# Layers 1 to 3 of a four-layer graph network on one core: whole-array vector passes against tile-by-tile ones over all eight PSUM banks

## The chip, the cores and the metric

The kernel runs on one core of a Trainium2 chip. The metric is the device time of one execution in microseconds (us), and the median of three runs is given. Engines are named as in the profile: PE is the matrix engine (PEld its weight loads), DVE the vector engine, ACT the scalar engine, POOL the GpSimd engine, SP the engine that only issues transfers here. PSUM, where PE writes, has eight banks of 512 floats on each of 128 partitions.

## The reference, cut to what matters

Four layers work on 3327 nodes with 128 features, in float32, all with the same dense 3327 x 3327 matrix `adj`. Each is x = x + layer(relu(layernorm(x))):

```
h = maximum(layernorm(x), 0);  x = x + L0(h, adj, adj, Wq, Wk, Wv, Wo)      # 128 "heads" of softmax attention
h = maximum(layernorm(x), 0);  x = x + L1(h, adj, embed, layer, biases)     # hyperbolic
h = maximum(layernorm(x), 0);  x = x + L2(h, adj, weight, bias)             # hyperbolic, with proj and relu
h = maximum(layernorm(x), 0);  x = x + L3(h, adj, W_in, W_out)

L1: a = f1(h @ embed); y = f2(a (+) embed_bias); u = adj @ y
    out = f3([h, f4(u)] @ layer) (+) layer_bias
L2: the same pattern: h @ weight.T, (+) bias, adj @ y, relu, rescaling
L3: (adj / rowsum(adj)) @ h @ W_in + (adj.T / rowsum(adj.T)) @ h @ W_out
a (+) b = ((1 + 2 a.b + b.b) a + (1 - a.a) b) / (1 + 2 a.b + a.a b.b), row by row
```

Every f multiplies a row by a number that depends on norms of the row alone (square roots, tanh, artanh).

## The kernel before

Node n = p*26 + t sits on partition p in tile t, so an array of all nodes is [128, 26, 128] and a number per node is [128, 26]. Layer 0 (lines 313 to 747) fills most of the time: its exponentials on ACT are in an order written out by hand, and it leaves its result in DRAM (`oT_d`) head by head. It is not part of the change. Everything from line 750 on is written without a fixed order: a scheduler places each instruction on its engine's queue, and each queue then runs in that order.

The end of layer 0 (lines 750 to 779, the output stage) loads `oT_d` two tiles at a time (`ot`, four buffers), divides by the softmax sums on DVE, transposes on PE, multiplies by `Wo`, and adds to `xs`, the array x. While it runs, the weights of the later layers and the first four strips of adj are loaded.

Layers 1 to 3 (lines 782 to 1006) hold every intermediate as a whole array and treat it in whole-array passes. `normed` (line 204) is the layer norm: a sum over each row, a subtraction, a square on ACT, a sum again, a multiplication and a maximum, each over 3328 elements per partition. `transposed` turns h over PE into `hT`, `project` (line 813) multiplies it with a weight, both four tiles at a time into the one bank `ps_t` that is left beside the seven of `aggregate`; `evac` copies each bank out, by ACT and DVE in turn. `sumsq` squares on ACT and sums on DVE. `ball_add` is (+): two passes for a.b, three for the result. `scaled` multiplies each row by its number. The numbers per node are worked out by `Small` in chains of 128x26 instructions on DVE, with square roots, tanh and logarithms on ACT.

`aggregate` (line 822) is adj @ y. Its seven banks collect [128 features, 3327 nodes] over 26 strips of adj, each a transfer of 1.66 MB into one of four buffers, issued by SP and POOL in turn; each strip meets y's tile as seven matmuls. Layer 1 and layer 2 call it once, layer 3 twice: first with the strips of adj transposed (`strip_T`), then with adj's rows (`strip_rows`). In layer 3 each strip is also summed on DVE for the degrees (line 836). Then the banks are copied out to `uT`, and `to_rows` (line 851) transposes back.

Of the kernel before, what the change touches and what calls it, by code (L numbers as in the profile page):

```python
# [10 lines left out]
F32 = mybir.dt.float32  # L11
# [11 lines left out]
P = 128  # L23
# [40 lines left out]
def tiles_of(b):  # L64
    return range(4 * b, min(4 * b + 4, NT))
# [18 lines left out]
def gnn_kernel(ctx: ExitStack, tc: tile.TileContext, x, adj, Wq, Wk, Wv, Wo, embed, layer,  # L84
# [665 lines left out]
    xs = load_x(const)  # L750
    with tc.tile_pool(name="f1", bufs=1) as f1, tc.tile_pool(name="f2", bufs=4) as f2, \
            tc.tile_pool(name="f_ps", bufs=3, space=PSUM) as f_ps:
        wo = f1.tile([P, HD], F32, name="wo")
# [27 lines left out]

    big = ctx.enter_context(tc.tile_pool(name="big", bufs=1))
    wts = ctx.enter_context(tc.tile_pool(name="wts", bufs=1))
    strips = ctx.enter_context(tc.tile_pool(name="strips", bufs=4))
    ps_u = ctx.enter_context(tc.tile_pool(name="ps_u", bufs=1, space=PSUM))
    ps_s = ctx.enter_context(tc.tile_pool(name="ps_s", bufs=1, space=PSUM))

    emb_w = wts.tile([P, D], F32, name="emb_w")
    nc.sync.dma_start(emb_w, embed)
    lay_w = wts.tile([P, 2, D], F32, name="lay_w")  # L790
    nc.sync.dma_start(lay_w, layer.rearrange("(k p) d -> p k d", p=P))
    w_in = wts.tile([P, D], F32, name="w_in")
    nc.sync.dma_start(w_in, W_in)
    w_out = wts.tile([P, D], F32, name="w_out")
    nc.sync.dma_start(w_out, W_out)
    w2T = weight_T(wts, ps_s, weight, "w2T")

    def on_all(v, name):
        o = wts.tile([P, D], F32, name=name)
        nc.sync.dma_start(o, v.unsqueeze(0).to_broadcast([P, D]))  # L800
        return o

    eb = on_all(embed_bias, "eb")
    lb = on_all(layer_bias, "lb")
    hb = on_all(bias, "hb")

    def arr(name):
        return big.tile([P, NT, D], F32, name=name)

    def matT():  # L810
        return big.tile([P, NP], F32, name="hT"), big.tile([P, NP], F32, name="uT")

    def project(lhsT, w, dst):

        for c in range(7):
            ts = tiles_of(c)
            ps = ps_s.tile([P, 4, P], F32, name="ps_t")
            for t in ts:
                nc.tensor.matmul(ps[:, t - 4 * c, :], lhsT[:, t * P:(t + 1) * P], w, start=True, stop=True)  # L819
            evac(dst[:, ts[0]:ts[-1] + 1, :], ps[:, :len(ts), :])  # L820

    def aggregate(y, uT, strip_of, deg=None):
# [3 lines left out]
        pu = [ps_u.tile([P, AW], F32, name=f"pu{c}") for c in range(7)]  # L826
# [10 lines left out]
        by_tile = uT.rearrange("f (t p) -> f t p", p=P)  # L837
        nc.vector.memset(uT[:, N:NP], 0.0)
        for c, w in enumerate(width):
            p0, k = c * AW // NT, w // NT  # L840
            evac(by_tile[:, :, p0:p0 + k], pu[c][:, :k * NT].rearrange("f (p t) -> f t p", t=NT))
        k *= NT
        evac(by_tile[:, 0:w - k, P - 1], pu[6][:, k:w])
# [7 lines left out]
    def to_rows(uT, dst):  # L851
        for c in range(7):
            ts = tiles_of(c)
            ps = ps_s.tile([P, 4, P], F32, name="ps_t")
            for t in ts:
                nc.tensor.transpose(ps[:, t - 4 * c, :], uT[:, t * P:(t + 1) * P], ident)
            evac(dst[:, ts[0]:ts[-1] + 1, :], ps[:, :len(ts), :])

    def scaled(dst, a, s):
        nc.vector.tensor_tensor(dst, a, over_d(s), op=ALU.mult)  # L860

    def row_sum(name, v, pool, tmp):

        o = pool.tile([P, 1], F32, name=name)
        nc.vector.tensor_tensor(tmp, v, v, op=ALU.mult)
        nc.vector.tensor_reduce(o, tmp, axis=AX.X, op=ALU.add)
        return o

    def ball_add(sm, dst, a, tmp, coef, norm, b, y2, least):

        nc.vector.tensor_tensor(tmp, a, over_t(b), op=ALU.mult)
        ab = sm.new()
        nc.vector.tensor_reduce(ab, tmp, axis=AX.X, op=ALU.add)
        xy = sm.mul(coef, ab)
        xn = sm.mul(coef, norm)
        x2 = sm.mul(xn, xn)
        e = sm.ts(xy, 2.0, ALU.mult, 1.0, ALU.add)
        na = sm.ts(e, y2[:, 0:1], ALU.add)
        den = sm.ts(sm.add(e, sm.ts(x2, y2[:, 0:1], ALU.mult)), least, ALU.max)
        rd = sm.recip(den)  # L880
        al = sm.mul(sm.mul(na, coef), rd)
        be = sm.mul(sm.ts(x2, -1.0, ALU.mult, 1.0, ALU.add), rd)
        nc.vector.tensor_tensor(tmp, over_t(b), over_d(be), op=ALU.mult)
        scaled(dst, a, al)
        nc.vector.tensor_tensor(dst, dst, tmp, op=ALU.add)

    brow = wts.tile([P, D], F32, name="brow")


    with tc.tile_pool(name="g1", bufs=1) as g1:  # L890
        sm = Small(g1, "s")
        eb2 = row_sum("eb2", eb, g1, brow)
        lb2 = row_sum("lb2", lb, g1, brow)
        h, tmp = arr("h"), arr("tmp")
        hT, uT = matT()
        normed(sm, xs, h, tmp)
        transposed(ps_s, h, hT)
        hh = sumsq(sm, h, tmp)
        nx = sm.ts(sm.sqrt(hh), L1_EPS, ALU.max)
        s1 = sm.div(sm.artanh(nx, L1_MAX_TANH), nx)  # L900
        a = arr("a")
        project(hT, emb_w, a)
        an = sm.sqrt(sumsq(sm, a, tmp))
        nv = sm.ts(sm.mul(s1, an), L1_EPS, ALU.max)
        c1 = sm.div(sm.mul(sm.act(nv, AF.Tanh), s1), nv)
        y = arr("y")
        ball_add(sm, y, a, tmp, c1, an, eb, eb2, L1_EPS)
        yn = sm.ts(sm.sqrt(sumsq(sm, y, tmp)), L1_EPS, ALU.max)
        scaled(y, y, sm.div(sm.artanh(yn, L1_MAX_TANH), yn))
        aggregate(y, uT, strip_T)  # L910
        u = arr("y")
        to_rows(uT, u)
        uu = sm.sqrt(sumsq(sm, u, tmp))
# [5 lines left out]
        w1, w2 = arr("a"), arr("y")  # L919
        project(hT, lay_w[:, 0, :], w1)  # L920
        project(uT, lay_w[:, 1, :], w2)
        scaled(w2, w2, cu)
        nc.vector.tensor_tensor(w1, w1, w2, op=ALU.add)
        wn = sm.sqrt(sumsq(sm, w1, tmp))
        nv2 = sm.ts(sm.mul(sz, wn), L1_EPS, ALU.max)
        c2 = sm.div(sm.mul(sm.act(nv2, AF.Tanh), sz), nv2)
        o1 = arr("y")
        ball_add(sm, o1, w1, tmp, c2, wn, lb, lb2, L1_EPS)
        nc.vector.tensor_tensor(xs, xs, o1, op=ALU.add)


    with tc.tile_pool(name="h1", bufs=1) as h1:
        sm = Small(h1, "s")

        def clip_of(n):

            return sm.ts(sm.recip(n), L2_MAXNORM, ALU.mult, 1.0, ALU.min)

        b2 = row_sum("b2", hb, h1, brow)
        b2w = sm.new()  # L940
        nc.vector.tensor_copy(b2w, b2.to_broadcast([P, NT]))
        bn = sm.ts(sm.sqrt(b2w), L2_MIN_NORM, ALU.max)
        bt = sm.act(bn, AF.Tanh)
        bc = sm.mul(sm.div(bt, bn), clip_of(sm.ts(bt, L2_MIN_NORM, ALU.max)))
        nc.vector.tensor_scalar(hb, hb, bc[:, 0:1], None, op0=ALU.mult)
        hb2 = row_sum("hb2", hb, h1, brow)

        h, tmp = arr("h"), arr("tmp")
        hT, uT = matT()
        normed(sm, xs, h, tmp)  # L950
        transposed(ps_s, h, hT)
        xn = sm.ts(sm.sqrt(sumsq(sm, h, tmp)), L2_MIN_NORM, ALU.max)
        a = arr("a")
        project(hT, w2T, a)
        an = sm.ts(sm.sqrt(sumsq(sm, a, tmp)), L2_MIN_NORM, ALU.max)
        th = sm.act(sm.mul(sm.div(an, xn), sm.artanh(xn, L2_MAX_TANH)), AF.Tanh)
        c1 = sm.mul(sm.div(th, an), clip_of(sm.ts(th, L2_MIN_NORM, ALU.max)))
        y = arr("y")
        ball_add(sm, y, a, tmp, c1, an, hb, hb2, L2_MIN_NORM)
        yn = sm.ts(sm.sqrt(sumsq(sm, y, tmp)), L2_MIN_NORM, ALU.max)  # L960
        pf = clip_of(yn)
        pn = sm.ts(sm.mul(yn, pf), L2_MIN_NORM, ALU.max)
        scaled(y, y, sm.mul(sm.div(sm.artanh(pn, L2_MAX_TANH), pn), pf))
        aggregate(y, uT, strip_T)
        u = arr("a")
        to_rows(uT, u)
        un = sm.ts(sm.sqrt(sumsq(sm, u, tmp)), L2_MIN_NORM, ALU.max)
        t1 = sm.ts(sm.act(un, AF.Tanh), L2_MIN_NORM, ALU.max)
        p2 = clip_of(t1)
        n2 = sm.ts(sm.mul(t1, p2), L2_MIN_NORM, ALU.max)  # L970
        k2 = sm.mul(sm.mul(sm.div(sm.artanh(n2, L2_MAX_TANH), n2), p2), sm.div(t1, un))
        nc.vector.tensor_scalar(u, u, 0.0, None, op0=ALU.max)
        rn = sm.ts(sm.mul(k2, sm.sqrt(sumsq(sm, u, tmp))), L2_MIN_NORM, ALU.max)
        t3 = sm.act(rn, AF.Tanh)
        k3 = sm.mul(sm.mul(sm.div(t3, rn), k2), clip_of(sm.ts(t3, L2_MIN_NORM, ALU.max)))
        scaled(u, u, k3)
        nc.vector.tensor_tensor(xs, xs, u, op=ALU.add)


    with tc.tile_pool(name="i1", bufs=1) as i1:  # L980
        sm = Small(i1, "s")
        h, tmp = arr("h"), arr("tmp")
        normed(sm, xs, h, tmp)
        vT, uT = matT()
        deg, degT = sm.new(), sm.new()
        nc.vector.memset(deg, 1.0)
        nc.vector.memset(degT, 1.0)
# [5 lines left out]
        aggregate(h, uT, strip_T, degT)  # L993
        aggregate(h, vT, strip_rows, deg)
        r_in, r_out = over_degree(deg), over_degree(degT)
        zi, zo = arr("a"), arr("y")
        project(uT, w_in, zi)
        project(vT, w_out, zo)
        scaled(zi, zi, r_in)
        scaled(zo, zo, r_out)  # L1000
        nc.vector.tensor_tensor(zi, zi, zo, op=ALU.add)
        nc.vector.tensor_tensor(xs, xs, zi, op=ALU.add)
        for p0, p1 in pieces(P - 1):
# [33 lines left out]
```

## Time and profile before

| what | us |
|---|---|
| median of 3 runs (lowest to highest) | 11689.48 (11686.55 to 11691.01) |
| the profiled execution's own time | 11686.64 |
| its span, first to last instruction | 11684.9 |
| layer 0 up to its last result store | 10572.9 |
| layer 0's output stage, to the last addition to `xs` | 103.3 |
| four aggregations, PE busy 294.2 in layers 1 and 2 and 292.5 in layer 3 | 586.7 in all |

The profiled execution is 2.8 us below the median. Its page lists the share of each engine over the whole span, of which layer 0 is nine tenths; the change is read from the last tenth, by stretches of time between the aggregations.

### The profile page before, as it was taken

The numbers are of one execution on the slowest core, as the hardware profiler recorded it, in microseconds if no ns is written. First come the engines' busy times: TensorE is split into PE (matmuls) and PEld (weight loads), VectorE is DVE, ScalarE is ACT, GpSimd is POOL, SyncE is SP. The second block draws the span as 40 slices with busy tenths as digits, with TensorE's granted clock in tenths as the row PEclk, the third lists the DMA queues.
The fourth block names the chain that finished last, engine by engine and source line by source line (L and its number), as shares of the span: only waits on it lengthen the run. The fifth ranks groups of instructions, "written<-read, shape, count | busy, mean of one in ns | idle before, by whom it ended". The sixth has DMA issues, their size and how long they took to land.

```text
span 11684.9 us, 195477 instructions
## 1 busy us (share of the span) xinstructions
PE 10973.1 (94%) x72798; PEld 3492.3 (30%) x72798; DVE 4850.4 (42%) x7190; ACT 10392.7 (89%) x13945; POOL 1887.6 (16%) x3247
## 2 busy tenths in 40 slices
PE   4699999999999999999999999999999999996578
PEld 2222222222222222222222222222222222224334
DVE  5344443444444443444444444444443333335335
ACT  3699999999999999999999999999999999993100
POOL 4211112111121111211112111121111211110000
PEclk7799999999999999999999999999999999997789
DMA  8755555555455544555555545455544544442356
GB/s 249 241 91 91 90 91 105 92 88 94 85 110 88 93 85 82 107 90 90 90 90 105 93 87 93 84 112 88 93 85 81 101 81 78 82 78 104 129 198 240
DMA packets 651406, 1242.72 MB, mean 106 GB/s; under 512 B 185527, under 2 KB 527424, under 8 KB 633820
## 3 DMA queue, kind: packets, MB, share of 16 engines
q1 hardware_dynamic: 609016, 1100.82, 48.4%
q0 software_dynamic: 41440, 129.30, 3.7%
q8 instruction: 588, 9.63, 0.4%
q14 instruction: 362, 2.97, 0.1%
HBM read 1082.90 MB, written 146.60 MB: 105 GB/s over the span
## 4 chain that ended last, share of the span: by engine, by line
ACT 80%; PE 8%; issue 5%; DVE 3%; DMA 1%; POOL 0%; SPq 0%; DVEq 0%; POOLq 0%; ACTq 0%
ACT e L641 80%; PE pu L833 5%; PE S L629 1%; PE ps_t L819 1%; PE po L649 1%; PE ps_y L778 0%; DVE S L623 0%; DVE s L201 0%; ACT tmp L199 0%; DMA ot<-oT_d 0%; DVE y L860 0%; PE ps_t L774 0%; DMA a<-adjT 0%; DVE s L149 0%; DMA QS<-qS_d 0%
## 5 line engine op out<-in xcount | busy, mean ns | idle before, releaser
L641 ACT ACTIVATE e<-S 128x952 f32<-128x952 f32 (+3 forms) x13589 | 10106.8, 916 | 8.9 <-PE S L629 7.8
L623 DVE COPY S<-a 128x476 f32<-128x476 f32 (+1 forms) x5824 | 3739.3, 655 | 5992.5 <-ACT e L641 5733.8
L649 PE MATMUL po<-e,VA 128*9 128x476 f32 (+1 forms) x46592 | 5738.7, 565 | 15.6 <-DVE OS L661 2.6
L629 PE MATMUL S<-QS,KT 64*128 64x476 f32 (+1 forms) x23296 | 5080.3, 443 | 111.2 <-DMA a<-adjT 18.8
L629 PEld LDWEIGHTS S<-QS,KT 64*128 64x128 f32 x23296 | 2277.8, 184 | 5376.8 <-DVE S L623 2703.1
L665 POOL DMA_DIRECT2D oT_d<-OS x896 | 470.7, 531 | 5599.7 <-DVE OS L661 5531.4
L649 PEld LDWEIGHTS po<-e,VA 128*9 128x9 f32 x46592 | 695.0, 89 | 1790.6 <-issue 1691.3
L550 POOL TENSOR_SCALAR QS<-QS 32x476 fp32r<-32x476 f32 (+1 forms) x1344 | 781.9, 582 | 1330.5 <-DMA QS<-qS_d 732.2
L123 ACT COPY uT<-pu 128x494 f32<-128x494 f32 (+2 forms) x12 | 6.3, 528 | 457.1 <-PE pu L833 456.5
L833 PE MATMUL pu<-strip,y 128*128 128x494 f32 (+2 forms) x728 | 294.2, 567 | 92.8 <-DVE y L860 92.8
L833 PE MATMUL pu<-strip,h 128*128 128x494 f32 (+2 forms) x728 | 292.5, 565 | 66.8 <-DVE h L213 66.8
L560 POOL COPY VA<-VR 128x832 f32<-128x832 f32 x224 | 198.4, 886 | 969.5 <-DMA VR<-v_d 740.9
L571 POOL TENSOR_TENSOR a<-a,shb 128x476 f32<-128x476 f32 (+1 forms) x182 | 213.0, 1205 | 240.4 <-DMA a<-adjT 203.9
L836 DVE TENSOR_REDUCE s<-strip 128x1 f32<-128x3327 f32 (+1 forms) x52 | 188.0, 3618 | 106.7 <-DMA strip<-adjT 60.6
L833 PEld LDWEIGHTS pu<-strip,y 128*128 128x128 f32 (+1 forms) x728 | 139.3, 192 | 247.1 <-issue 142.2
L275 DVE STREAM_TRANSPOSE cols<-rows 128x416 f32<-128x416 f32 x208 | 203.5, 983 | 21.0 <-DMA rows<-in_adj_dram 14.1
L833 PEld LDWEIGHTS pu<-strip,h 128*128 128x128 f32 (+1 forms) x728 | 138.9, 191 | 220.2 <-issue 141.1
L661 DVE COPY OS<-po 128x476 f32<-128x476 f32 (+1 forms) x224 | 145.6, 650 | 52.3 <-PE po L649 45.9
L831 POOL DMA_DIRECT2D strip<-adjT x39 | 20.7, 532 | 791.9 <-PE pu L833 764.0
L123 ACT COPY hT<-pu 128x494 f32<-128x494 f32 (+1 forms) x4 | 2.2, 546 | 143.0 <-PE pu L833 143.0
L221 PE MATMUL ps_t<-ident,h 128*128 128x128 f32 x78 | 20.3, 428 | 114.9 <-DVE h L213 100.9
L127 DVE COPY uT<-pu 128x494 f32<-128x494 f32 (+2 forms) x12 | 6.8, 577 | 290.8 <-PE pu L833 290.4
(153 smaller groups left out, 1745.5 us busy)
## 6 DMA issues: line engine op xcount, KB each, us to landing
KT<-kS_d SPq DMA_DIRECT2D x1792, 208.0 KB
KT<-kS_d SPq DMA_DIRECT2D x1792, 104.0 KB
VR<-v_d SPq DMA_DIRECT2D x224, 416.0 KB
strip<-adjT POOLq DMA_DIRECT2D x39, 1663.5 KB, 7.6
strip<-adjT SPq DMA_DIRECT2D x36, 1663.5 KB
QS<-qS_d SPq DMA_DIRECT2D x3072, 14.9 KB
QS<-qS_d SPq DMA_DIRECT2D x1536, 29.8 KB
adjT<-cols SPq DMA_DIRECT2D x26, 1664.0 KB
```

Of the source, the lines that this page charges most:

```text
L275: nc.vector.transpose(self.cols[:, t0:t0 + NQ, 32 * j:32 * j + 32], self.rows.rearrange("p (x t) -> p t x", t=NT)[:, t0:t0 + NQ, :])
L550: nc.gpsimd.tensor_scalar(QS[b][r0:r0 + 32, j + 1, :w], QS[b][r0:r0 + 32, j, :w].bitcast(F32), -1.0, 0.0, op0=ALU.mult, op1=ALU.add)
L560: nc.gpsimd.tensor_copy(VA[(c * NG + g) % 2][:, :, :, 0:H], v.rearrange("p j (t e) -> p t j e", e=H))
L571: nc.gpsimd.tensor_tensor(a[:, :w], a[:, :w], shift[:, :w], op=ALU.subtract)
L623: touch(u, [r], nc.vector.tensor_copy(bank(u, r), adj_of[c][2 * q + r][:, :w]))
L629: x = nc.tensor.matmul(bank(u, r), KT[b][64 * r:64 * r + 64, max(0, j - 1), q * P:(q + 1) * P], QS[b][64 * r:64 * r + 64, j, :w], start=Fa ...
L641: touch(u, range(a, b), nc.scalar.activation(e[:, a:b, :w], S[u % 3][:, lo + a:lo + b, :w], AF.Exp, scale=2.0))
L649: nc.tensor.matmul(po[32 * j:32 * j + H + 1, :w], VA[k % 2][:, 2 * q + r, j, :], e_of[u, j][:, at, :w], start=(q == 0 and r == 0), stop=(q ...
L661: nc.vector.tensor_copy(o[:, :w], po[:, :w])
L665: nc.gpsimd.dma_start(oT_d[:, d * N + c * CW:d * N + c * CW + w], o[32 * j:32 * j + H + 1, :w])
L833: nc.tensor.matmul(pu[c][:, :w], y[:m, t, :], s[:m, c * AW:c * AW + w], start=(t == 0), stop=(t == NT - 1))
L836: nc.vector.tensor_reduce(deg[:m, t:t + 1], s[:m], axis=AX.X, op=ALU.add)
```

## The change

It rewrites layers 1 to 3 and moves their preparations ahead of layer 0's output stage. Part by part:

- Weights and biases are loaded, and all that depends on the biases alone is computed, before the output stage. `embed`, `layer` and `weight` get one more column, the product with the bias (`with_product`), so that a.b comes out of the projection.
- `layer_norm` replaces `normed`: per tile `bn_stats` and `bn_aggr` on DVE, then per tile one ACT instruction relu(r*x + off).
- All eight banks are shared by `bank_u`: projections and transposes rotate over seven, the eighth takes norms. Squares are summed over features by a matmul with a column of ones (`column_squares`), or per three or four tiles (`row_squares`).
- (+) and the scalings become per-tile instructions `scalar_tensor_tensor` (`add_scaled`), and the norm of the sum is computed from numbers per node (`sum_norm`) rather than from the array.
- h @ layer[:128] is projected before layer 1's aggregation; the sums of the strips in layer 1 give `degT`; layer 3 takes adj's rows first, and the projection of that result runs inside its second aggregation, by `also`.
- The last projection, the addition to x and the store go in seven groups.

```diff
+    eb, lb, hb = on_all(embed_bias, "eb"), on_all(layer_bias, "lb"), on_all(bias, "hb")
+    ...
+        bc = sm.mul(sm.div(bt, bn), clip_of(sm, sm.ts(bt, L2_MIN_NORM, ALU.max)))
+        nc.vector.tensor_scalar(hb, hb, bc[:, 0:1], None, op0=ALU.mult)
+    emb_w = wts.tile([P, D + 1], F32, name="emb_w")
+    ...
+        with_product(lay_w[i], lb)
+    with_product(emb_w, eb)
+    ...
+        w_raw = f1.tile([P, D], F32, name="w_raw")
+        nc.sync.dma_start(w_raw, weight)
+        ...
         wo = f1.tile([P, HD], F32, name="wo")
...
-    ps_u = ctx.enter_context(tc.tile_pool(name="ps_u", bufs=1, space=PSUM))
-    ps_s = ctx.enter_context(tc.tile_pool(name="ps_s", bufs=1, space=PSUM))
+    banks_u = ctx.enter_context(tc.tile_pool(name="banks_u", bufs=1, space=PSUM))
+    def next_bank():
+        turn[0] += 1
+        return bank_u(turn[0] % 7)
+    def layer_norm(sm, xs, h):
+        mv = sm.pool.tile([P, NT, 2], F32, name="mv")
+        for t in range(NT):
+            st = part.tile([P, 6], F32, name="st", bufs=8)
+            nc.vector.bn_stats(st, xs[:, t, :])
+            nc.vector.bn_aggr(mv[:, t, :], st)
+        r = sm.recip(sm.sqrt(sm.ts(mv[:, :, 1], LN_EPS, ALU.add)))
+        off = sm.mul(sm.ts(mv[:, :, 0], -1.0, ALU.mult), r)
+        for t in range(NT):
+            nc.scalar.activation(h[:, t, :], xs[:, t, :], AF.Relu, scale=r[:, t:t + 1], bias=off[:, t:t + 1])
+    def column_squares(sm, of, dst_of=None):
+        o = sm.new()
+        ps = bank_u(7)
+        for c in range(7):
+            ts = tiles_of(c)
+            src = of(c)
+            sq = part.tile([P, 4 * P], F32, name="sq")
+            nc.scalar.activation(sq[:, :len(ts) * P], src, AF.Square)
+            if dst_of is not None:
+                nc.vector.tensor_copy(dst_of(c), src)
             for t in ts:
+                nc.tensor.matmul(ps[:, t:t + 1], sq[:, (t - ts[0]) * P:(t - ts[0] + 1) * P], ones,
+                                 start=True, stop=True)
+        nc.vector.tensor_copy(o, ps[:, :NT])
+        return o
+    def add_scaled(dst, a, s, b):
+        nc.vector.scalar_tensor_tensor(dst, a, s, b, op0=ALU.mult, op1=ALU.add)
...
-        y = arr("y")
-        ball_add(sm, y, a, tmp, c1, an, eb, eb2, L1_EPS)
-        yn = sm.ts(sm.sqrt(sumsq(sm, y, tmp)), L1_EPS, ALU.max)
-        scaled(y, y, sm.div(sm.artanh(yn, L1_MAX_TANH), yn))
-        aggregate(y, uT, strip_T)
+        al, be = ball_sum(sm, c1, aa, ab, eb2, L1_EPS)
+        yn = sm.ts(sum_norm(sm, al, be, aa, ab, eb2), L1_EPS, ALU.max)
+        f = sm.div(sm.artanh(yn, L1_MAX_TANH), yn)
+        al, be = sm.mul(al, f), sm.mul(be, f)
+        y = arr("y")
+        for t in range(NT):
+            nc.scalar.activation(y[:, t, :], a[:, t, 0:D], AF.Copy, scale=al[:, t:t + 1])
+            add_scaled(y[:, t, :], eb, be[:, t:t + 1], y[:, t, :])
+        w1 = arr("w", D + 1)
+        project(hT, lay_w[0], lambda ts, ps: evac(w1[:, ts[0]:ts[-1] + 1, :], ps))
+        pu, width = aggregate(y, strip_T, degT)
...
-        ball_add(sm, o1, w1, tmp, c2, wn, lb, lb2, L1_EPS)
-        nc.vector.tensor_tensor(xs, xs, o1, op=ALU.add)
+        al, be = ball_sum(sm, c2, ww, w1[:, :, D], lb2, L1_EPS)
+        for t in range(NT):
+            add_scaled(xs[:, t, :], w1[:, t, 0:D], al[:, t:t + 1], xs[:, t, :])
+            add_scaled(xs[:, t, :], lb, be[:, t:t + 1], xs[:, t, :])
...
-        aggregate(h, uT, strip_T, degT)
-        aggregate(h, vT, strip_rows, deg)
-        ...
-        project(uT, w_in, zi)
-        project(vT, w_out, zo)
-        scaled(zi, zi, r_in)
-        scaled(zo, zo, r_out)
-        nc.vector.tensor_tensor(zi, zi, zo, op=ALU.add)
-        nc.vector.tensor_tensor(xs, xs, zi, op=ALU.add)
+        r_out = over_degree(degT)
+        pu, width = aggregate(h, strip_rows, deg)
+        vT = matT("hT")
+        by_tiles(pu, width, vT)
+        r_in = over_degree(deg)
+        pu, width = aggregate(h, strip_T, also={
+            3 * c + 4: lambda c=c: add_projected(c, bank_u(7), vT, w_out, r_out) for c in range(7)})
+        uT = matT("uT")
+        by_tiles(pu, width, uT)
+        for c in range(7):
+            add_projected(c, next_bank(), uT, w_in, r_in)
+            ...
+            nc.sync.dma_start(out[0:(P - 1) * NT].rearrange("(p t) d -> p t d", t=NT)[:, ts[0]:ts[-1] + 1, :],
+                              xs[0:P - 1, ts[0]:ts[-1] + 1, :])
```

`ball_sum` and `sum_norm` are some fifteen and ten 128x26 instructions; `add_projected` is four matmuls into one bank and four `add_scaled` into xs.

## The prediction

> **What bounds the kernel now.** The page's first lines say ACT 89% and PE 94%, but nine tenths of the span are layer 0, which the change leaves alone. So I first cut the span at the aggregations (busy time in nine stretches), then asked for the groups of instructions by form after layer 0, for the chain of waits, and last for PE's granted clock in short stretches.
>
> ```profile
> core 0: us, PE busy (x) PEld busy (x) DVE busy (x) ACT busy (x) POOL busy (x), PEclk, DMA share, GB/s
> 10572.90:10676.20 103.30, 78.89 (x633) 75.41 (x633) 75.32 (x88) 17.09 (x28) 10.32 (x13) 0.87 0.66 227
> 10676.20:10777.40 101.20, 21.05 (x78) 16.21 (x78) 68.25 (x114) 24.95 (x24) 0.00 (x0) 0.51 0.00 0
> 10777.40:10924.80 147.40, 147.25 (x364) 69.69 (x364) 2.02 (x3) 1.80 (x4) 6.93 (x13) 0.99 0.81 287
> 10924.80:11116.00 191.20, 54.92 (x208) 43.48 (x208) 126.11 (x227) 49.48 (x54) 0.00 (x0) 0.51 0.03 11
> 11116.00:11263.00 147.00, 146.93 (x364) 69.63 (x364) 2.04 (x4) 1.76 (x3) 6.87 (x13) 0.99 0.81 288
> 11263.00:11340.50 77.50, 5.56 (x26) 3.41 (x26) 59.71 (x84) 18.65 (x18) 0.00 (x0) 0.54 0.07 25
> 11340.50:11633.00 292.50, 292.48 (x729) 139.16 (x730) 179.05 (x65) 3.93 (x7) 12.69 (x24) 0.99 0.77 280
> 11633.00:11685.00 52.00, 20.23 (x105) 16.94 (x103) 19.34 (x13) 4.33 (x8) 0.00 (x0) 0.64 0.10 33
> ```
>
> Read it by rows: in the aggregations PE is busy all the time, so nothing but PE sets their length. In the gaps between them (101.2, 191.2, 77.5, 52.0, together 422 us) no engine is full. DVE leads with 60 to 77%, and the rest is one engine waiting for the other. The change is about these 422 us and the 103 us of the output stage before them. The prices:
>
> ```profile
> L201 DVE TENSOR_REDUCE s<-tmp 128x26 f32<-128x3328 f32 x13 | 47.0, 3619 | 30.9 <-ACT tmp L199 30.9
> L149 DVE TENSOR_TENSOR s<-s,s 128x26 f32<-128x26 f32 x142 | 25.2, 182 | 3.9 <-ACT s L176 0.3
> L199 ACT ACTIVATE tmp<-y 128x3328 f32<-128x3328 f32 x3 | 8.9, 2976 | 27.2 <-DVE y L885 27.1
> L860 DVE TENSOR_TENSOR y<-y,s 128x3328 f32<-128x3328 f32 x4 | 14.5, 3625 | 0.5 <-ACT y L123 0.3
> L779 DVE TENSOR_TENSOR xs<-xs,ps_y 128x128 f32<-128x128 f32 x26 | 7.4, 285 | 7.2 <-PE ps_y L778 7.1
> L176 ACT ACTIVATE s<-s 128x26 f32<-128x26 f32 x28 | 6.3, 225 | 56.2 <-DVE s L161 44.6 <-DVE s L149 11.5
> ```
>
> A whole-array pass costs 3.62 us on DVE and 2.98 on ACT; a tile costs 0.285 on DVE, so 26 tiles 7.4, twice the pass. Tiles win only where they remove passes or let engines overlap. Dependent 128x26 steps start 0.22 us apart in the timeline; a step over ACT and back takes 0.47.
>
> ```profile
> 10714.00:10732.00 18.00, 13.63 (x52) 11.63 (x52) 2.15 (x4) 1.75 (x3) 0.00 (x0) 0.50 0.01 1
> 10777.40:10781.00 3.60, 3.55 (x5) 1.61 (x6) 0.00 (x0) 0.00 (x0) 0.00 (x0) 0.50 0.00 0
> 10781.00:10785.00 4.00, 4.00 (x12) 1.97 (x11) 0.00 (x0) 0.00 (x0) 0.00 (x0) 1.00 0.00 0
> 11633.00:11645.30 12.30, 7.47 (x54) 6.13 (x52) 2.46 (x6) 2.58 (x5) 0.00 (x0) 1.00 0.00 1
> ```
>
> PE's clock: a projection at 76% busy stays at half clock (2.08 us for four tiles), 3.6 us without a pause bring full clock (1.16), and once there 61% busy keeps it.
>
> **1. Output stage, earlier ready time.** Before, PE starts its first `ot` at 10592.7, stalls from 10603 to 10616 for later `ot` loads, then runs full at 5.57 us for two tiles. After, by the order of the queues: SP issues eight small transfers first (about 5.5 us by their rows before), then `ot`, strip, `ot`, strip, `w_raw`, `wo`; on POOL's queue too a strip now stands before the second `ot`. PE's first instruction is the transpose of `w_raw`, whose memory is that of the bias chain's numbers, so its load waits for the scaling of `hb` on DVE; that stands behind the sum of the first strip (3.62), which waits for that strip. Four strips, four `ot` and weights are 12 MB; the stretch 10574 to 10600 moved about 0.39 MB per us, so they are in by about 10607. PE starts at 10608. The stall at the fifth `ot` is then gone, since four are there. PE alone would end at 10608 + 13 x 5.57 = 10680. DVE has more: nine pairs of reciprocal and product 36.3 (1.75 + 2.28), 26 copies 15.6, 26 additions 6.5, three strip sums 10.7, the products with the biases 2.5, and 26 pairs of `bn_stats` and `bn_aggr`. These last are not in the trace. Nearest row: a 128x128 sum, 0.28, and a small step, about 0.12 when it waits for nothing: 0.40, so 10.4. Bounds: 0.2 (both hidden in each other's start) and 1.0 (three passes over a tile). Sum 82 us, 10690, and 5 for the last pair's way through PE: statistics complete at 10695.
>
> **2. Layer 1 up to its aggregation.** Small chain 3.0. Then 26 relus on ACT with two per-partition operands. The rows give (2976 - 225)/3302 = 0.83 ns an element, so 0.31 a tile, 8.1 in all. [...] At 10708 the squares can start (they follow the relus in ACT's queue), and hT's copies follow the squares. From here PE has ones (52 loads and matmuls), `emb_w` and `layer` (52 each): 21.5 us at full clock (0.127 an instruction with one column, 0.29 a tile), 39.5 at half. DVE has 7 copies, 9 copies of a, 9 sums, 33 small steps, 5 copies of w: 22. The small steps after the norm of a stand in DVE's queue behind the last copy of w, so all of this counts. PE has no pause at half clock and should warm up; I take 27, between 22 and 39.5. Then square root 1.7, tanh and c1 1.6, `ball_sum` 2.4, `sum_norm` 1.3, square root and artanh 5.5 (6.0 before from 10767.8 to 10773.8). That is 12.5. The first aggregation waits for y's first tile only, 0.9, where before it waited for three whole passes. Start: 10695 + 3 + 10.4 + 27 + 12.5 + 0.9 = 10749, against 10777.4. **-28.**
>
> **3. Between aggregations 1 and 2** (191.2 before), counted from the last matmul: copies out 1.0; square and ones 7.3, numbers to `cu` 2.7 (sum 11); DVE then has 26 `add_scaled` 7, 9 sums 4.1, about 45 small steps 7: 18 (29); last square and sum 1, chain to `al` 5.5 (35.5); 52 `add_scaled` on xs at 0.27, 14 (49.5); statistics 10.4 (60); chain 3 (63); relus 10.4 (73.4); first square, ones and projection with DVE's 14 us beside, 19.6 (93); artanh of h's norm, clips and the chains of layer 2, 19 (112); y 0.9 (113). What goes: six squares and sums (6.6 each), two `ball_add` with five passes each, the passes of `normed`, and h @ `layer`, which now lies before the aggregation. **-78.**
>
> **4. Between 2 and 3** (77.5): copies out 1; transposes, relu, 14 squares on ACT at 0.54 and the ones 12 (13); chain 13, as before from 11286 to 11299; `add_scaled` 7 (33); statistics 10.4 (43.4); small chain 3 and, in its midst in DVE's queue, the sums of the first four strips, 14.1, exactly as before: here nothing is gained, as adj's rows come first and need their own degrees (60.5); first relu and matmul 0.9 (61.4). **-16.**
>
> **5. The aggregations.** 26 projections inside the last one: 26 x 0.29 at full clock, **+7.5**. The strip sums of layer 1, 22 x 3.62 = 80 us of DVE, lie beside 147 us of PE, where DVE had 2 us of work; a buffer is free when both have read it, and DVE reads earlier. Cost nothing; layer 3 before shows the same sums under PE at 292.48 of 292.50. If DVE came late, POOL and SP would issue strips late and PE would wait: see the rivals.
>
> **6. End** (from PE's last matmul to the end 51.8): copies out 1.0, first group 1.2, 26 additions at 0.3, 7.8, last transfer 3.8 (7.8 before from the last issue, of which 1.7 MB at the rate above are 4.4): 14. POOL's seven one-partition stores go beside. **-38.**
>
> Sum: -28 - 78 - 16 + 7.5 - 38 = -152.5. From the profiled execution's own 11686.6: 11534. The median of the runs shown stands 2.8 above it: **11537**.
>
> **Rivals.** (a) PE stays at half clock in the projections: 39.5 for 27 in layer 1, about +8.5 in layer 2: 11537 + 21 = 11558. [...] (b) The output stage is later, since a load is held by in-order DVE: every us that `wo` comes after 10608 is a us; with `ot`s also queued behind strips, +20: 11557. (c) All overlaps are good: `bn` 0.25, layer 1 bound by DVE's 22, output stage 6 earlier: about 11512. (d) The statistics take 1.0 a tile, 78 tiles: +47, 11584. (e) Slower: the fixed price of a small instruction. About 338 per-tile instructions stand one after another on the path (26 relus and 52 statistics in layer 1's start, 156 in gap 3, 78 in gap 4, 26 at the end), reckoned at some 0.3. From 0.75 us each the 152 us are eaten; at 0.8 the time is about 11706. Against it stand 26 rows of 0.285 at the same size on DVE; for it, that two-tensor forms with a per-partition scalar are not in the trace at this size.
>
> **How the numbers follow.** Likeliest 0.47, (a) 0.17, (b) 0.1, (c) 0.15, (d) 0.08, (e) 0.03. Own range of the likeliest: 11520 to 11552 (10 us on the output stage, 6 on `add_scaled`, 8 on the clock). With (a), (b), (c) and most of (d): 11505 to 11582. This kernel's measurement can tell about 0.2%, 23 us, from no change; only (e) comes near, so faster 0.96, same 0.015, slower 0.025.
>
> **What would show it.** Right: gaps of about 113 and 61 us before PE's second and third aggregation, the first starting near 10749, PE still full inside all four, the last additions 10 us behind PE's last matmul, `bn` pairs near 0.4 and relus near 0.4. Wrong: pauses of PE inside the first aggregation, a granted clock of 0.5 through all projections, `add_scaled` above 0.4 us, or an output stage that ends after 10710.

## The result, and the profile after

The changed kernel takes 11600.4 us (median of 4 runs, 11598.5 to 11601.2), the kernel before 11689.0 (11686.6 to 11691.0): a ratio of 0.9924, 95% interval 0.9907 to 0.9941. That is 88.6 us faster where 152 were forecast; the time lies 63 us above the forecast and 18 above the upper end of its range. The profiled execution took 11601.2 us, with a span of 11599.4.

The span is cut at the aggregations as before; each row gives the busy time of each engine in one stretch (columns in the first line). The stretches between aggregations are called gaps.

```profile
core 0: us, PE busy (x) PEld busy (x) DVE busy (x) ACT busy (x) POOL busy (x), PEclk, DMA share, GB/s
10574.60:10702.50 127.90, 79.16 (x633) 74.73 (x633) 103.34 (x179) 20.36 (x33) 10.32 (x13) 0.83 0.53 183
10702.50:10758.10 55.60, 38.22 (x182) 32.10 (x183) 28.85 (x129) 27.94 (x60) 0.00 (x0) 0.62 0.00 1
10758.10:10906.60 148.50, 148.42 (x364) 69.97 (x364) 88.81 (x50) 8.61 (x28) 6.96 (x13) 0.98 0.80 285
10906.60:11017.60 111.00, 47.19 (x235) 41.04 (x235) 71.35 (x350) 44.37 (x86) 0.00 (x0) 0.58 0.05 18
11017.60:11166.00 148.40, 148.39 (x364) 69.94 (x364) 9.17 (x28) 8.60 (x27) 6.90 (x13) 0.98 0.80 285
11166.00:11227.70 61.70, 14.34 (x79) 14.02 (x79) 46.99 (x169) 16.71 (x28) 0.00 (x0) 0.56 0.09 32
11227.70:11526.20 298.50, 298.47 (x780) 144.35 (x780) 92.01 (x60) 13.47 (x32) 12.75 (x24) 0.99 0.76 274
11526.20:11599.40 73.20, 6.07 (x52) 5.88 (x52) 7.08 (x28) 0.45 (x1) 3.44 (x7) 0.56 0.06 24
```

The two gaps between aggregations are what was forecast, 111.0 and 61.7 us, and PE is full in all aggregations. The last row is the surprise: 73.2 us after PE's last matmul of the aggregations, against 51.8 before and 14 forecast. No engine does anything in most of it: PE has 6 us, DVE 7. By step, the differences add up to the change of the span: start of the first aggregation 10777.4 to 10758.1, -19.3; gaps -80.2 and -15.8; aggregations +8.5; end +21.4; together -85.4 of the 85.5.

The stretch after the last addition, and the transfers to `out` by their queue (durations in ns as least, median, most, then the first and last start):

```profile
11535.20:11599.40 64.20, 0.00 (x0) 0.00 (x0) 0.00 (x0) 0.00 (x0) 0.49 (x2) 0.50 0.06 25
```
```profile
L1113 SPq DMA_DIRECT2D out_dram<-xs x7: 241/10061/10129, 11529.3 to 11574.4; - x7
L1115 POOL DMA_DIRECT2D out_dram<-xs x7: 484/487/517, 11529.6 to 11535.2; - x7
```

POOL has issued its seven one-partition stores by 11535.7. SP's seven stand 10.06 us (median) in the queue. The DMA share is 0.06, one sixteenth, and it is the mean busy share of 16 engines: that could be one engine that is always busy, or sixteen that are seldom busy. The trace's packet records tell which. Of the 67.8 us in which SP's queue moves packets, exactly one packet is in flight for 64.3, and never more than two; a packet of 2 KB takes 79 ns. So one engine carries 25 GB/s and fifteen stand still. 254 KB a group at that rate is the 10 us that each store takes. Before, the same 1.7 MB left in 8.6 us, with sixteen packets in flight for most of the transfer:

```profile
11676.30:11684.90 8.60, 0.00 (x0) 0.00 (x0) 0.00 (x0) 0.00 (x0) 0.00 (x0) 0.50 0.61 198
```

What differs is the first dimension of the transfer. The kernel before stores 112 and then 15 partitions (`pieces`); the change stores 127 at once. The experiments ask first whether it is that, or POOL's stores, or the smaller pieces; then what sets the rest of the time.

### The profile page after: what moved, and what is told of

Read it like the earlier page. It is cut to its first block, busy times and chain, and to the rows that moved or that the text cites. A ratio compares the mean times of both kernels' runs of the same rounds, so it can differ in the third digit from the quotient of the medians.

```text
span 11599.4 us, 196522 instructions
## 1 busy us (share of the span) xinstructions
PE 10982.6 (95%) x72980; PEld 3500.4 (30%) x72980; DVE 4766.2 (41%) x7583; ACT 10411.4 (90%) x14091; POOL 1895.5 (16%) x3254
## 4 chain that ended last, share of the span: by engine, by line
ACT 80%; PE 8%; issue 6%; DVE 2%; DMA 1%; POOL 0%; SPq 0%; DVEq 0%; POOLq 0%; ACTq 0%
ACT e L641 79%; PE pu L941 5%; PE S L629 1%; PE po L649 1%; DVE S L623 0%; PE pu L893 0%; DMA ot<-oT_d 0%; PE ps_y L837 0%; DVE xs L928 0%; PE pu L916 0%; PE pu L904 0%; POOL a L571 0%; DVE s L149 0%; DMA KT<-kS_d 0%; DVE s L944 0%
## 5 line engine op out<-in xcount | busy, mean ns | idle before, releaser
L275 DVE STREAM_TRANSPOSE cols<-rows 128x416 f32<-128x416 f32 x208 | 203.2, 982 | 21.4 <-DMA rows<-in_adj_dram 14.1
L407 ACT CAST st_k<-st_q 128x1664 fp32r<-128x1664 f32 x16 | 53.7, 3378 | 75.9 <-DMA st_q<-kraw_d 58.0
L944 DVE TENSOR_REDUCE s<-strip 128x1 f32<-128x3327 f32 (+1 forms) x26 | 93.9, 3616 | 59.7 <-DMA strip<-in_adj_dram 59.7
L944 DVE TENSOR_REDUCE degT<-strip 128x1 f32<-128x3327 f32 (+1 forms) x26 | 94.0, 3616 | 54.0 <-DMA strip<-adjT 54.0
## 6 DMA issues: line engine op xcount, KB each, us to landing
QS<-qS_d SPq DMA_DIRECT2D x3072, 14.9 KB
```

Of the source, the lines that this page charges most:

```text
L275: nc.vector.transpose(self.cols[:, t0:t0 + NQ, 32 * j:32 * j + 32], self.rows.rearrange("p (x t) -> p t x", t=NT)[:, t0:t0 + NQ, :])
L944: nc.vector.tensor_reduce(deg[:m, t:t + 1], s[:m], axis=AX.X, op=ALU.add)
```

## The experiments

All times are medians of four runs; the kernel before measured 11689.3, 11688.3 and 11689.1 beside the three groups of four.

**1. The store cut at 112** (`e1_split_store`).

```diff
-            nc.sync.dma_start(out[0:(P - 1) * NT].rearrange("(p t) d -> p t d", t=NT)[:, ts[0]:ts[-1] + 1, :],
-                              xs[0:P - 1, ts[0]:ts[-1] + 1, :])
+            for p0, p1 in pieces(P - 1):
+                nc.sync.dma_start(out[p0 * NT:p1 * NT].rearrange("(p t) d -> p t d", t=NT)[:, ts[0]:ts[-1] + 1, :],
+                                  xs[p0:p1, ts[0]:ts[-1] + 1, :])
```

> The changed kernel, but each of the seven stores to `out` on SP's queue is cut at partition 112 (112 and 15 partitions) as all other transfers of 127 partitions in the kernel are. Theory A (a transfer whose first dimension is 127 goes to one DMA engine, so the last 73 us are 1.69 MB at 24 GB/s): the stores keep up with the additions, the last work is POOL's last one-partition store, landing about 5 us after 11535; time about 11541 us, 59 below the changed kernel. Theory B (POOL's seven one-partition stores are what ends late): no change, 11600. Theory C (seven store groups of 2 KB pieces instead of one with 13 KB pieces are slow in themselves, and there are now fourteen): 11600 or later.

Measured: 11541.5 us (11540.0 to 11543.9), ratio to before 0.9873 (0.9857 to 0.9890). Its end, in two stretches:

```profile
11526.20:11535.20 9.00, 6.07 (x52) 5.88 (x52) 6.81 (x26) 0.00 (x0) 3.43 (x7) 0.98 0.40 117
11535.20:11540.40 5.20, 0.00 (x0) 0.00 (x0) 0.00 (x0) 0.00 (x0) 0.00 (x0) 0.50 0.42 132
```

The last matmul of its aggregations ends at 11525.4, so the end is now 15.0 us long, with POOL's stores and the 2 KB pieces still there. Theories B and C fall; 59 of the 63 us that were missing are in this one line of code.

**2. The kernel before, with its two stores of 112 and 15 made one of 127** (`e2_before_127`).

```diff
-        for p0, p1 in pieces(P - 1):
+        for p0, p1 in ((0, P - 1),):
```

> The kernel before with one edit: its store of 112 and its store of 15 partitions at the end become one store of 127 partitions (13 KB per partition); the one-partition store stays. Theory A: 1.69 MB at 24 GB/s, 66 to 70 us from the issue at 11676.3 instead of 8.6, so 57 to 62 us slower than before, 11746 to 11751, ratio about 1.005. Theories B and C: no change, since POOL has no store here and the pieces are as long as before.

Measured: 11745.5 us (11743.1 to 11751.6), ratio 1.0049 (1.0032 to 1.0065), 56 us slower than before, for the 57 to 62 of theory A: A again, from the other side. Its last stretch:

```profile
11678.70:11744.50 65.80, 0.00 (x0) 0.00 (x0) 0.00 (x0) 0.00 (x0) 0.00 (x0) 0.50 0.06 26
```

One engine again, with pieces of 13 KB: the length of the pieces is not it.

**3. The cut at 124** (`e3_124_3`): the edit of 1 with `((0, 124), (124, 127))` for `pieces(P - 1)`.

> As the changed kernel with the seven stores cut at partition 124 (124 and 3 partitions). [...] By this rule each of the seven groups takes 254 KB at 4 x 24 = 97 GB/s, 2.6 us, more than the 1.03 us between two groups: end at about 11529 + 17.8 + 2 = 11549, so about 11551 us, 49 below the changed kernel and some 10 above the cut at 112. Rival A2 (whatever is not a multiple of 16 goes to one engine): 11600. Rival A3 (only a prime number is slow, all others take 16 engines): 11541.

Measured: 11554.3 us (11552.6 to 11557.5), ratio 0.9885 (0.9869 to 0.9902); 13 above the cut at 112, 46 below the changed kernel. Busy share in tenths and GB/s of the transfers in 40 slices from 11529 to the end:

```profile
DMA  0222222222331222222222222222222221000000
GB/s 11 75 62 87 83 100 102 102 105 77 81 59 26 55 86 86 79 97 100 107 100 100 107 100 100 107 100 100 103 100 100 75 73 48 5 0 0 14 0 0
```

A quarter of the engines, at most 107 GB/s, four times 25; four packets are in flight for 14 of 20.6 us. A2 and A3 both fall. The expectation's four engines for 124, its "4 x 24", were an assumption that no earlier run shows; with it the forecast of 11551 is right to 3 us. The packets of SP's queue can also be counted. Seven stores of 127 rows are 889 packets of data, and beside them stand 7 packets of 4 bytes in the changed kernel, 49 = 7 x (4 + 3) with the cut at 124, and 217 = 7 x (16 + 15) with the cut at 112. Read as one per engine and store, which is a reading, that is one engine for 127, four and three for 124 and 3, sixteen and fifteen for 112 and 15. What was in flight at once fits it for three of them: one packet for 127, four for 124, and sixteen in the kernel before, whose stores of 112, 15 and 1 have 32 = 16 + 15 + 1 such packets.

**4. Store once, as before** (`h1_store_once`): the changed kernel with the loop's stores taken out and the three stores of the kernel before after the loop.

> The changed kernel with the end of the kernel before: no store in the loop of additions, and after it the three stores of 112, 15 and 1 partitions. From the changed kernel's trace the last addition ends at about 11534.9; from there 8.6 us as before: span 11543.6, time about 11545, some 3.5 above the cut in seven groups. So the overlap of stores and additions is worth 3 to 4 us if the cut is right. Rival: nothing at all (below 1 us), as the last group's store still has to be issued and to land.

Measured: 11543.2 us (11542.2 to 11544.8); from PE's first matmul of the last projection to the end 2.3 us more than with seven cut groups, by the two profiles. The ranges of the two times overlap. So letting stores and additions overlap is worth about 2 us at best, and its uncut form cost 57.

**5. Weights first** (`e5_weights_first`): experiment 1, and

```diff
+    w_raw = wts.tile([P, D], F32, name="w_raw")
+    nc.sync.dma_start(w_raw, weight)
+    wo = wts.tile([P, HD], F32, name="wo")
+    nc.sync.dma_start(wo, Wo)
     eb, lb, hb = on_all(embed_bias, "eb"), on_all(layer_bias, "lb"), on_all(bias, "hb")
...
-        w_raw = f1.tile([P, D], F32, name="w_raw")
-        nc.sync.dma_start(w_raw, weight)
...
-        wo = f1.tile([P, HD], F32, name="wo")
-        nc.sync.dma_start(wo, Wo)
```

> The cut at 112, and `w_raw` and `wo` in memory of their own, loaded first on SP's queue in the output stage, ahead of the biases, so that PE no longer waits for DVE's bias chain (in the changed kernel PE stood still from 10574 to 10612). Theory (each us that PE starts earlier in the output stage is a us, until DVE's own 103 us of work fill it): the first transposes of `ot` start near 10596 instead of 10616, DVE has no idle time after its first `ot`, statistics complete about 7 us earlier, time about 11534 (7 below the cut alone). Rival (DVE's work or the landing of the `ot` loads already sets the end of the stage): within 2 us of the cut alone.

Measured: 11542.2 us (11540.4 to 11546.3), no gain. By one profile each, PE's first `ot` comes 17.5 us after layer 0's last copy instead of 42.7, but layer 1's first relu 127.2 after it instead of 129.1. The rival holds: PE's start is not what sets the stage's end. (Part of the missing gain lies elsewhere: see the gap at the end of experiment 7.) Its trace has POOL's later `ot` loads wait 58.9 us for PE to let a buffer go.

**6. Degree sums of the first four strips, later.** Tied to the first tile of the aggregation's left side, in layer 3 (`f1_late_sums_l3`), in layer 1 (`f2_late_sums_l1`), and in both with early weights (`f3_late_weights`) or without (`g1_both_ties`), each on top of experiment 1:

```diff
             if deg is not None:
+                if t < 4:
+                    nc.vector.tensor_copy(deg[:m, t:t + 1], y[:m, 0, 0:1])
                 nc.vector.tensor_reduce(deg[:m, t:t + 1], s[:m], axis=AX.X, op=ALU.add)
```

> The cut at 112, and in layer 3 the sums of the first four strips of adj's rows are tied to the first tile of h: one element of h is copied into the sum's place first, so that DVE can't take them up in the midst of the layer norm's small steps. Theory (step 4 of the prediction: these 14.1 us stand on the path between aggregations 2 and 3): gap of 47 to 48 us instead of 61.6, time about 11527, 14 below the cut alone. Rival (the layer norm's way over ACT or PE's clock sets the gap, and DVE would wait in that time anyway): gap above 58, within 4 us of the cut alone.

> The cut at 112, and in layer 1 the sums of the first four strips of adj's columns are tied to the first tile of y in the same way, so they leave the output stage and lie beside PE's first aggregation. Theory (DVE's own work sets the end of the output stage, which is why earlier weights brought nothing): DVE's busy time there falls from 103 to 89 us, `w_raw` and `wo` come 3.6 us earlier, first relu 8 to 14 us earlier, time 11528 to 11534. Rival (the loads of `ot` pace the stage): within 3 us of the cut alone. Check on the cost: PE must stay full in the first aggregation, 148.4 us.

> Both ties (layers 1 and 3), and `w_raw` and `wo` loaded first. If DVE sets the output stage, the early weights bring something only together with the late sums: DVE then has 89 us of work from about 10590, and waits for the third `ot`, which lands behind four strips near 10605. Theory: 14 from layer 3, 14 to 18 from the output stage against the cut alone: 11510 to 11514. Rival (weights early bring nothing with or without the sums): the sum of the two single changes, 11514 to 11520.

> The cut at 112 and both ties of degree sums (layers 1 and 3), weights as in the changed kernel. The single ones measured -12.3 and -3.4 us against the cut alone. Theory 1 (the early weights of the kernel with both ties cost as much as the tie in layer 1 brought): the two add up, about 11525 to 11526. Theory 2 (the 3.4 of layer 1 were chance in the order of the queues): 11529, as with the tie of layer 3 alone.

Measured, against the 11541.5 of experiment 1: layer 3 alone 11529.2 (11526.0 to 11531.9), -12.3; layer 1 alone 11538.1 (11534.4 to 11541.2), -3.4; both 11526.6 (11524.0 to 11528.6), -14.9, about the sum; both with early weights 11531.2 (11530.2 to 11531.9), -10.3, worse than both without them and outside both of its expectations. The groups of runs come from different chips, on which the kernel before differs by 1 us. For layer 3 the cause shows in DVE's timeline of the changed kernel (start, duration in us), just before the third aggregation:

```profile
11211.21 3.61 DVE L944 TENSOR_REDUCE s<-strip 128x1 f32<-128x3327 f32 x1
11215.17 3.61 DVE L944 TENSOR_REDUCE s<-strip 128x1 f32<-128x3327 f32 x1
11218.95 3.60 DVE L944 TENSOR_REDUCE s<-strip 128x1 f32<-128x3327 f32 x1
11222.83 3.60 DVE L944 TENSOR_REDUCE s<-strip 128x1 f32<-128x3327 f32 x1
```

and in that of the kernel with the tie:

```profile
11209.95 0.27 DVE L945 COPY s<-h 128x1 f32<-128x1 f32 x3 [0.56 <-ACT h L874]
11210.15 10.66 DVE L946 TENSOR_REDUCE s<-strip 128x1 f32<-128x3327 f32 x3
```

In the first, four sums stand between the layer norm's small steps and hold back the relus. In the second they begin 0.2 us after PE's aggregation (11209.98) and lie beside it. The second aggregation's start to the third's is 197.6 us instead of 210.1. In layer 1, 14 us less of DVE's work in the output stage brought 3.4 us alone and 2.5 beside the other tie, with ranges that overlap. In its one profile the first relu stands 7.8 us earlier than in that of experiment 1; but `f1_late_sums_l3`, whose output stage has the code of experiment 1, shows it 5.8 earlier as well, so single profiles of this stage spread by that much and the times decide. DVE's amount of work sets at most a small part of it. PE stays full in the first aggregation (148.3 us with both ties).

**7. Which load comes first in the output stage.** Strips after tile 6 of xs (`f4_all`, with the last row's stores on SP); six buffers for `ot` with early weights (`g2_six_ot_weights`); six buffers alone (`g3_six_ot`), where the strips' memory falls on the output stage's and they load after the last `ot`:

```diff
 # f4_all, on top of f3_late_weights
+            if deg is degT and t < 4:
+                nc.vector.tensor_copy(s[:, 0:1], xs[:, 6, 0:1])
 # g2_six_ot_weights, on top of f3_late_weights; g3_six_ot, on top of g1_both_ties
-            ot = f2.tile([P, H + 1, 2 * P], F32, name="ot")
+            ot = f2.tile([P, H + 1, 2 * P], F32, name="ot", bufs=6)
```

> As the one with both ties and early weights, and two things more: the first four strips' loads wait for tile 6 of xs (one element of it is copied into each strip first), so that four `ot` on each queue go ahead of 6.7 MB of strips; and the last row's seven stores go on SP's queue instead of POOL's. Theory: the 12 us that PE and DVE spend waiting for the third and later `ot` shrink to 4; the end comes 1 to 2 us earlier; about 11502. Rival (DVE's work is contiguous already, or a strip's load now comes too late for the first aggregation): within 3 us of the one before, or later.

> Both ties, early weights, and six buffers for `ot` instead of four. In the kernel with both ties and early weights DVE waited 12.5 us for loads of `ot` between 10600 and 10702 and PE 24 us for DVE, because a load is issued only when PE has let a buffer go and lands 6.7 us later. Theory (the four buffers set the pace of the output stage): stage 8 to 12 us shorter, about 11520. Rival (the order of DVE's queue sets it): within 3 us of 11531.

> Both ties, weights as in the changed kernel, six buffers for `ot`. Here the strips' memory falls on that of the output stage, so the first strips' loads stand behind the last `ot` on both queues and the first six `ot` meet no strip in the DMA engines. Theory (buffers, and strips ahead of `ot`, set the pace): `w_raw` and `wo` still come behind the bias chain, but near 10592 instead of 10607; first relu near 10685 instead of 10700; about 11515. Rival (the strips now land too late for the first aggregation, or DVE's order sets the pace): 11525 or later.

Measured: 11534.4 (11531.2 to 11536.2), 11528.3 (11524.9 to 11529.5) and **11518.3** (11515.1 to 11520.7). `f4_all` misses its expectation by 32 us. DVE's waits for `ot` between 10600 and 10702 did not shrink from 12 us to 4, and POOL's queue stood 12.6 us at a strip that waits for DVE, with the next `ot` load behind it (us in total, times, longest):

```profile
DVE rc L825 <- DMA ot<-oT_d: 14.7, 4, 8.4
...
POOL strip L941 <- DVE strip L939: 12.6, 1, 12.6
```

Six buffers with early weights are 2.9 us below the same kernel with four, at the edge of what the ranges can part. Six buffers with the weights late and all strips behind the last `ot` are 8.3 below the same with four, and their ranges are apart, though the two profiled executions differ by only 3.3. Here the strips are issued from 10687 on, land before the first aggregation, and layer 1's first relu comes 116.7 us after layer 0's last copy (122.1 with four buffers, by one profile each). `w_raw` was issued at 10601.8, 10 us later than expected, and still the stage was shorter: again PE's start was not the point. Buffers and strip order changed together here, so which of the two brought the 8 us stays open.

Both kernels with six buffers, `f4_all` and `e5_weights_first` also show 114.5 to 114.6 us for the gap after the first aggregation, against 111.0 to 111.3 in the other changed kernels. The granted clock (the figure after POOL's) tells where the 3.5 us go. Three us of this gap, from 4 us after the aggregation's last matmul on, first in the changed kernel and then in `e5_weights_first`:

```profile
10910.52:10913.52 3.00, 3.00 (x30) 3.00 (x28) 0.00 (x0) 1.58 (x3) 0.00 (x0) 1.00 0.63 262
```
```profile
10907.38:10910.38 3.00, 3.00 (x16) 3.00 (x16) 0.00 (x0) 1.18 (x2) 0.00 (x0) 0.50 0.60 248
```

In these four PE falls to half clock about 4 us after the aggregation instead of 7.7, so the sums of squares that the one-column matmuls build are ready 15.6 us after it instead of 12.2. Why the clock falls earlier there stays open. The times of these four hold these 3.5 us, which are not the output stage's.

The kernel `g3_six_ot` is the fastest: ratio to before 0.9853 (0.9836 to 0.9869), 171 us, and 82 below the changed kernel.

## Why the prediction was wrong, and where it was right

**The step that failed is 6, the end.** "Last transfer 3.8" took the rate of the kernel before, whose store has a first dimension of 112, for a store with one of 127. In its place 64.4 us pass from the last addition, at 11535.0, to the end, on one DMA engine. The rest of the step is right to 1 us: with the cut at 112 the end is 15.0 us, by the forecast's 14. Of the 67 us by which the change of the span was overrated, 59 are in this step (-38 forecast, +21.4 measured) and 9 in steps 1 and 2. The runs show 25 GB/s for 127, at most 107 for 124, and 198 as a mean over the last 8.6 us of the kernel before, with 112 and 15. An estimate after the fact, from the measured 25 GB/s: 1.69 MB take 68 us from the first store, 3 us after PE's last aggregation matmul: 71 for 14, and the sum would have been 11594. The signs were in the code: `pieces` cuts the loads of x and of adj's strips wherever they have 127 partitions, and the diff drops that cut in the stores to `out`. The rivals of the prediction had no slow transfer among them. That POOL's stores "go beside" was right.

**Step 1, the output stage:** the first `ot` came at 10616.2 for 10608 and the statistics were complete 125.5 us after layer 0's last copy, for 122 forecast. Some 3 us are within what single profiles of this stage spread. But the step adds DVE's work to PE's start, and neither acts so. Rival (b), "every us that `wo` comes after 10608 is a us", is refuted: 25 us earlier brought 2. And 14 us less of DVE's work brought 3.4. So that 122 came near is in part luck, and what sets the stage's end stays open. The `bn` pairs stand 0.26 us apart, not 0.40, within the bounds. The transfers of the kernel before moved 365 GB/s from 10574 to 10600, where the forecast has 0.39 MB per us.

**Step 2, layer 1:** 58.0 us from complete statistics to the first aggregation for 53.8. The mis-sized term is the 27 for the projections:

```profile
10713.20:10720.00 6.80, 6.80 (x32) 6.80 (x33) 3.61 (x6) 2.70 (x5) 0.00 (x0) 0.50 0.01 2
10720.00:10727.00 7.00, 7.00 (x33) 7.00 (x34) 0.76 (x2) 0.38 (x1) 0.00 (x0) 0.50 0.00 1
10727.00:10734.00 7.00, 7.00 (x38) 7.00 (x37) 5.97 (x25) 2.02 (x5) 0.00 (x0) 0.55 0.00 1
10734.00:10743.70 9.70, 7.32 (x59) 6.55 (x57) 7.46 (x31) 4.77 (x10) 0.00 (x0) 1.00 0.01 2
```

PE (first busy column) has no pause from 10713 on and still runs at half clock until about 10733.3 (the third row's mean of 0.55), 20 us of the 30.5 that the block takes. So rival (a) was right for two thirds of the block. Beside the relus the clock did not rise either: from 10703 to 10713 PE was busy with transposes for 9.91 of 10 us, at a granted clock of 0.50. "PE has no pause at half clock and should warm up" rests on the 3.6 us in the aggregation before, and on a projection that kept full clock at 61% busy. Neither carries over to this block, which mixes projections with the one-column matmuls on `ones`. In the gap after the first aggregation PE even lost full clock, at about 10914.3, while it had no pause:

```profile
10913.00:10914.00 1.00, 1.00 (x11) 1.00 (x11) 0.00 (x0) 0.85 (x2) 0.00 (x0) 1.00 0.13 53
10914.00:10915.00 1.00, 1.00 (x7) 1.00 (x7) 0.00 (x0) 0.85 (x1) 0.00 (x0) 0.63 0.06 27
10915.00:10916.00 1.00, 1.00 (x8) 1.00 (x6) 0.00 (x0) 0.00 (x0) 0.00 (x0) 0.50 0.00 0
```

In layers 1 and 2 full clock came about 5 us after the last one-column matmul (10727.9 and 10733.3; 10991.0 and 10996.1). Whether these matmuls hold the clock down stays open; no run takes them away. The forecast's 0.127 us for an instruction with one column was the author's estimate; at half clock these stand 0.21 apart. Its 10.4 us for 26 relus, 0.40 each, in layers 1 and 2 are shown by no run before the change, whose rows gave 0.31. In layer 1 the 26 took 10.13 us, 0.39 each, while the scaling of y with one per-partition operand in place of two takes 7.70, 0.30 each.

**Steps 3 and 4:** 111.0 for 113 and 61.7 for 61.4. The sums are better than their terms, and that is luck. In step 4 transposes, squares and ones end 21.4 us after the aggregation, for 13, as the 52 one-column matmuls take 11.3 us at half clock (granted clock 0.50):

```profile
11176.00:11187.40 11.40, 11.25 (x52) 11.16 (x52) 0.24 (x3) 4.91 (x9) 0.00 (x0) 0.50 0.00 0
```

The statistics (6.9 for 10.4), the chain before them (10.1 for 13) and the one behind them (16.0 for 17.1) take it back. In step 3 the first square, ones and projection of layer 2 take 25.0 for 19.6, PE again busy without a pause at half clock for 20 us (10976.3 to 10996.1); there too the statistics (6.9 for 10.4) and the last chain (16.0 for 19) make up for it. That in the gap before the third aggregation four strip sums stand "in its midst in DVE's queue" and cost 14.1 us was right in kind: taking them out gave 12.3 us. **Step 5:** +8.5 for +7.5; strip sums under the aggregations cost nothing, as said.

## What to carry to other kernels

Read the first dimension of every transfer that a diff touches, not only its bytes: a duration or a rate from another row holds only for the same shape (here 198 GB/s with 112 and 15 partitions, 25 with 127), and where a kernel cuts a dimension in a helper, a line that leaves the helper out is a change of its own. Here a DMA share of 0.06 in a stretch where no engine works was one DMA engine of 16, and about 0.25 was four. In the output stage neither PE's earlier start nor less work on DVE bought more than 4 us; sums of 14 us in the midst of a small chain cost 12 of them.

## What was not expected of the hardware

One DMA engine alone moved 25 to 26 GB/s, whether the pieces were 2 or 13 KB long; the cut store of 13 KB pieces moved 198 as a mean over its last 8.6 us, in which the engines were busy for 0.61. PE without a pause kept half clock for 20 us in layer 1 (10713 to 10733), where before the change 3.6 us in the first aggregation had been enough. POOL's one-partition stores took 4.8 us to land (median) beside the uncut transfers and 2.7 beside the cut ones, and 7.3 beside those at 124.
